# A message-passing layer with a sorted edge list: layernorm's products rebooked, the loop's vector work planned, gathers further ahead

## The chip, the cores and the metric

The kernel runs on one core of a Trainium2 chip. The metric is device microseconds (us) for one execution. TensorE is written PE here, VectorE DVE, ScalarE ACT, GpSimd POOL and SyncE SP. PE, DVE, ACT, POOL and SP each work through their own list of instructions in order; a semaphore makes one wait for another. The program order within each engine is the order in which the Python code emits the instructions.

## The reference

```python
h = jnp.maximum(_layernorm(x, axis=-1), 0.0)          # x: 6250 nodes x 128
feat = jnp.concatenate([h[dst], h[src] - h[dst]], axis=-1)
msg = feat @ W.T + b                                  # one message an edge, 206250 edges
out = jax.ops.segment_max(msg, dst, num_segments=6250)
x = x + jnp.where(jnp.isfinite(out), out, 0.0)
```

The edges are sorted by dst. They are two random lists of 100000, each with its reverse, and one loop edge a node. A message splits into a part of dst and a part of src, so the kernel computes two products a node (a part that is added to the output and the table Bt, which is to be maximised over a node's sources) and then takes the maximum of rows of Bt over each node's edges.

## The kernel before, in words

**Layout.** There are 128 lanes of 49 consecutive nodes (LD = 49). Each lane reads a window of 1792 edges (WIN), and nodes are also split as node = 50 l + q (Q = 50 and L = 125). Most of the edges are handled by matrix products with one-hots; those left over, edges whose (dst, q) occurs a second time in a lane, are handled as a stream of rows, 396 steps of 128 rows (GR = 396), one row a lane and step.

**Stage 1, loads (0 to 29 us).** The windows of src and dst are gathered, x is loaded in five groups of ten q (GQ = 10). `scaled` (L511) normalises two q on ACT into one of two buffers `hs`.

**Stage 2, the list's sums (29 to 109 us).** For 41 lags DVE compares each edge's key with that of the edge `lag` places before (L608), and PE adds the result into the PSUM tile `dup` (L597, four matmuls); five more sums mark edges before, in and behind the lane. Three buffers hold the compared lists, so DVE runs at most three ahead of PE. Into this the code strews layernorm: 75 parts (`micro`), three a pair of q: `turn` (transpose on PE, copy on ACT to `hT`, then normalise the next pair), `product` (a bias matmul and two f32 matmuls, L527 and L530, with two copies on ACT, L532 and L533) and `remainder` (one matmul L539, one copy L541, and for each fifth pair the store of Bt by SP, L545, and the adding store into out by POOL, L546). `ln(2)` emits two parts after each lag. `moments` and `scales` compute the statistics, `put_x` (L674) has SP copy raw x to out.

**Stage 3, marking and sorting (109 to 165 us).** ACT takes signs of `dup`, DVE scans them (L707), and eleven passes (`pass_`, L644 and L645: a test and a predicated copy) move the left-over edges to the front of each lane. Beside the passes the list `rest` says what is emitted after which pass: `turned` moves the three per-edge names into the layout of T3 (TQ, TD, TV), a quarter of the lanes at a time (14 or 28 matmuls of 32 columns, then a copy, L762); `build` compares names with row numbers into the first two units' homes (`pieces`, L203, L207, L210: six pieces a unit) and multiplies them into `pv` (`mats`, L242); `own_last` counts; `begin_rows` (after pass 7) computes the first indices `ridx` (L790) and issues LEAD = 16 row gathers. Then DVE closes the list, SP writes it to LT, POOL gathers from LT by `cols_` the rows that fuller lanes hand over, and DVE computes limits and checks.

**Stage 4, the loop (from 177 us).** A new pool takes over the memory of stages 1 to 3's pool. 13 tiles of ten lanes (490 columns; the last has 392) times 25 pairs of q give 325 pairs. A pair is: two to four one-hot products on PE (L955) turned into ones by ACT (L956), made one pair ahead; four or six f32 products into `ps` (L1046, two buffers); a maximum on DVE (L1052, or L1050 for a tile's first pair). `plan` holds, by tile and pair, the batches of `mats`, `feats` and `put_own` for the next tile, and `between` the pieces of the unit after the next. `more_rows` spreads the 396 steps of the row stream evenly over the first 291 pairs: a step (`stream_step`, L170) is a running maximum on DVE; after each, one more row is gathered (`gather_row`, L91) by POOL, made to wait for that step, so 16 rows are ahead; the ring in X holds 42 rows (GB = 7 groups of U = 6), and each full group is written by SP to M. From pair 112 on (`find_ends`), each third step also lets POOL gather a row R of ends out of M (32 by pair 291, 17 later). The last 34 pairs hold the finishing of the output.

## Time and profile before

| | us |
|---|---|
| median of three runs (805.58 to 807.24) | 806.66 |
| the profiled execution's own time | 804.5 |
| its span, first to last instruction | 802.8 |
| busy: PE, DVE, ACT, POOL | 684.5, 705.7, 554.7, 471.0 |
| mean granted clock of PE | 0.956 |

The profile lists, for one execution, when each instruction ran on its engine. A row of a timeline is: start, duration, engine, line, operation, output<-input, shape, count, and in brackets how long the engine sat idle before it and what released it. A row of a group has busy time and mean ns. A row of the waits is: who waited for whom, us in total, times, longest. PE's time is union time of overlapping matmuls, so a busy PE is not one at its peak.

### The profile page before, as it was taken

Reading aid. Unit: us, or ns where it says so; the run is one execution under the profiler, and the core shown is the slowest. Engines: PE = TensorE matmul, PEld = TensorE weight load, DVE = VectorE, ACT = ScalarE, POOL = GpSimd, SP = SyncE. Lnnn points to the kernel's source line nnn. Section 1 sums busy time; section 2 is a strip of 40 time slices with the busy share of each in tenths; the row PEclk is TensorE's granted clock in tenths of the full one; section 3 lists DMA queues with packets and bytes.
Section 4 is the critical chain, followed back from the end, with each engine's and each line's share of the span. In section 5 each row is a group of like instructions: output and inputs, shape, how many; then the busy total and the mean of one; then the engine's idle time right before and its main releaser. Section 6 shows DMA issues by size and latency. Waiting matters only on the chain.

```text
span 802.8 us, 12579 instructions
## 1 busy us (share of the span) xinstructions
PE 684.5 (85%) x3992; PEld 515.2 (64%) x3992; DVE 705.7 (88%) x1256; ACT 554.7 (69%) x1168; POOL 471.0 (59%) x519
## 2 busy tenths in 40 slices
PE   0599955509999899999989999999999989899995
PEld 0366635307767677776767777676777756667894
DVE  7997589937999898999989999999999888898885
ACT  4878942325887988889776776768676675666863
POOL 4001010363767676767767777777777777777372
PEclk9999977559999999999999999999999999999998
DMA  6845430021343343433333333333433333343137
GB/s 188 256 98 106 88 78 2 14 76 39 92 116 88 86 121 89 115 89 99 108 84 104 108 102 108 106 108 94 120 94 109 105 105 89 92 119 92 56 74 141
DMA packets 79653, 79.43 MB, mean 99 GB/s; under 512 B 10042, under 2 KB 68495, under 8 KB 79579
## 3 DMA queue, kind: packets, MB, share of 16 engines
q0 software_dynamic: 16560, 37.64, 18.5%
q1 hardware_dynamic: 62667, 40.30, 17.6%
q8 instruction: 33, 0.54, 0.3%
q10 hardware_dynamic: 352, 0.61, 0.3%
q14 instruction: 41, 0.34, 0.1%
HBM read 39.25 MB, written 39.19 MB: 98 GB/s over the span
## 4 chain that ended last, share of the span: by engine, by line
PE 44%; DVE 18%; ACT 13%; DMA 11%; issue 9%; POOL 3%; DVEq 0%; SPq 0%; POOLq 0%; ACTq 0%
PE ps L1046 22%; PE z L955 10%; DMA X<-Bt,ridx 8%; DVE acc L1052 7%; ACT oh L956 5%; PE pv L242 5%; DVE X L170 2%; PE dup L597 2%; POOL X L91 2%; PE pm L530 2%; DVE dwin L645 2%; ACT Vb L257 1%; ACT dump L1080 1%; DVE big L644 1%; ACT acc L533 1%
## 5 line engine op out<-in xcount | busy, mean ns | idle before, releaser
L91 POOL DMA_INDIRECT X<-Bt,ridx x396 | 390.7, 987 | 192.4 <-DVE X L170 59.5
L956 ACT ACTIVATE oh<-z 126x490 fp32r<-126x490 f32 (+1 forms) x754 | 381.7, 575 | 153.7 <-PE z L955 151.6
L1046 PE MATMUL ps<-oh,Bp 126*128 126x490 f32 (+1 forms) x1508 | 439.5, 419 | 19.1 <-DVE acc L1052 18.4
L1052 DVE TENSOR_TENSOR acc<-acc,ps 128x980 f32<-128x980 f32 (+1 forms) x312 | 359.8, 1153 | 38.0 <-PE ps L1046 34.1
L1046 PEld LDWEIGHTS ps<-oh,Bp 126*128 126x128 f32 x1508 | 281.4, 191 | 103.0 <-DVE acc L1052 43.4
L955 PE MATMUL z<-Vb,Sel 128*126 128x490 f16 (+1 forms) x650 | 195.3, 371 | 29.6 <-ACT oh L956 24.6
L170 DVE SCALAR_TENSOR_TENSOR X<-X,slim 128x128 f32<-128x128 f32 x395 | 136.2, 345 | 11.6 <-DMA X<-Bt,ridx 10.6
L955 PEld LDWEIGHTS <-Sel 128*126 128x126 f16 x754 | 99.4, 139 | 63.6 <-issue 29.7
L242 PEld LDWEIGHTS <-OHQ 128*128 128x128 bf16 x840 | 58.5, 161 | 19.3 <-issue 18.6
L203 DVE TENSOR_TENSOR OHQ<-T,IQ 128x1092 bf16<-128x1092 bf16 (+5 forms) x96 | 57.3, 600 | 12.4 <-DMA X<-LT,cols__1131 12.4
L242 PE MATMUL pv<-OHD,OHQ 128*128 128x28 bf16 (+1 forms) x826 | 62.2, 228 | 5.7 <-DVE OHD L210 5.7
L91 POOL DMA_INDIRECT R<-M,last_e x49 | 48.8, 995 | 20.0 <-issue 8.8
L546 POOL DMA_DIRECT2D out_x<-acc x10 | 8.5, 984 | 81.5 <-ACT Bp L541 42.8
L955 PE MATMUL z<-Vf,Sel 128*126 128x490 f16 (+1 forms) x104 | 38.7, 372 | 0.5 <-ACT Vf L257 0.5
L597 PE MATMUL dup<-T,identb 128*128 128x512 bf16 (+1 forms) x164 | 37.0, 353 | 0.0
L608 DVE TENSOR_TENSOR T<-KA,KB 128x1792 bf16<-128x1792 int16 x21 | 22.8, 1091 | 15.9 <-PE dup L597 15.9
L1080 ACT ACTIVATE dump<-lane_dl,nbias 128x472 bf16<-128x472 int32 x50 | 35.1, 702 | 0.1
L530 PE MATMUL pm<-wT,hT 128*125 128x256 f32 x100 | 26.2, 384 | 0.0
L597 PEld LDWEIGHTS <-identb 128*128 128x128 bf16 x164 | 15.1, 98 | 14.0
L511 ACT ACTIVATE hs<-X,nmr,rstd 125x128 f32<-125x128 f32 x50 | 22.4, 508 | 0.5 <-DMA M<-none 0.5
L608 DVE TENSOR_TENSOR T<-KA 128x1792 bf16<-128x1792 int16 x20 | 21.2, 1075 | 1.2 <-PE dup L597 1.1
L645 DVE COPY_PREDICATED dwin<-big,dwin 128x472 int32<-128x472 int32 (+10 forms) x12 | 21.8, 1818 | 0.4
(298 smaller groups left out, 511.8 us busy)
## 6 DMA issues: line engine op xcount, KB each, us to landing
M<-X SPq DMA_DIRECT2D x66, 384.0 KB
X<-Bt,ridx POOLq DMA_INDIRECT x396, 2.5
X<-in_x SPq DMA_DIRECT2D x5, 560.0 KB
out_x<-X SPq DMA_DIRECT2D x5, 560.0 KB
Bt<-acc SPq DMA_DIRECT2D x5, 560.0 KB
out_x<-acc POOLq DMA_DIRECT2D x5, 560.0 KB, 9.0
ownb<-Bt SPq DMA_DIRECT2D x11, 245.0 KB
out_x<-R POOLq DMA_DIRECT2D x5, 480.0 KB, 9.9
```

What stands on the lines that cost most here:

```text
L91: i = G_.indirect_dma_start(out=o, out_offset=None, in_=table, in_offset=bass.IndirectOffsetOnAxis(ap=idx, axis=0))
L170: step = V.scalar_tensor_tensor(G[:, j], state["prev"], slim[:, k:k + 1], G[:, j], op0=ALU.min, op1=ALU.max)
L203: V.tensor_tensor(OHQ[:, :nl, a:z], over(TQ, z - a), iq, ALU.is_equal)
L242: last = T_.matmul(o, w, m, start=False, stop=True, skip_group_check=True)
L530: T_.matmul(pm[:L, j], hT[k % 2][:, j, :L], wT, start=False, stop=j == 1)
L597: T_.matmul(dup[:, a:z], w, e[:, a:z], start=first, stop=last)
L608: V.tensor_tensor(e, KA[:, 64:], i1, ALU.is_equal)
L955: T_.matmul(z[:L + 1, :n], Sel[:, order[i // 2][j]], f[t % 2][:, :n], start=True, stop=True)
L956: A_.activation(oh[:, :n], z[:L + 1, :n], AF.Relu)
L1046: T_.matmul(ps[:, j, :n], w, o[:, :n], start=m == 0, stop=m == len(todo) - 1)
L1052: V.tensor_tensor(a, a, ps[:, :, :n], ALU.max)
L1080: A_.activation(dump, lane_dl, AF.Sign, scale=2.0, bias=nbias[:, c:c + 1], accum_out=ends[:, c:c + 1])
```

## The change

- **Bookings of layernorm.** Before, two parts follow each lag. After, one part comes ahead of the distances' absolute value and four ahead of the first sum; within the sums a budget of PE time (`ln_spare`, 0.15 us a lag and 0.3 to 2.0 us more at ten lags) decides; the rest come after ACT's signs (18) and after passes 0, 1, 2 (6, 8, 8) and 3 (what is left). Groups 1 to 4 are normalised in place in X, one pair a lag at most (`scale_more`), so `put_x` is emitted earlier. ACT's copies of swin and KA move to lags 3, 7 and 11; its copies of `dup` and of the names move behind the products.
- **Names.** `turned` now takes all 128 lanes at once, 14 blocks in the four banks of `dup`, with two copies; TD and TV after pass 4, TQ after pass 5. Clearing and the load of the first own rows come after pass 5, the four `own_last` after pass 6, both builds and the first features after passes 7 and 8. The homes of units 0 and 1 change places in `acc`.
- **Gathers.** LEAD is 20: three after pass 7, then one behind each DVE piece of the builds and passes 8 to 10. R0 is 32. In the loop a step gathers one row, each eighth step two, until 36 are ahead (AHEAD) or the ring is full.
- **Planned steps.** The code now keeps a reckoning of each engine's time (`tm`) from durations written in, and after each pair emits row steps and pieces until DVE's reckoned time meets PE's next pair; a row may be up to 12 ahead of its even spread if it is reckoned to have landed, and is forced when 5 behind.
- **Pools.** `cols_` moves to the pool that stays for the whole kernel. The first one-hots are emitted before the padding copies and the third unit's pieces. `handed` moves from pair 5 to pair 11.

```diff
-R0 = 24
+R0 = 32
-LEAD = 16
+LEAD = 20
+AHEAD = 36
...
+            cols_ = keep.tile([P, 1], I32, name="cols_")
...
-            at_ = 2 * (Q * (L + 1)) - (UL + TL - UL) * (SQ + WN) * NBLK
+            at_ = 2 * TL * LD
-            for u_ in (0, 1):
+            for u_ in (1, 0):
...
+                def normal(k):
+                    return hs[k % 2] if 2 * k < GQ else xs[:, 2 * k:2 * k + 2]
...
-                    if k + 1 < NP_:
+                    if 2 * (k + 1) < GQ:
                         scaled(k + 1)
+                def scale_more():
+                    if GQ <= 2 * ready["s"] < 2 * ready["n"]:
+                        scaled(ready["s"])
...
-                            micro.append((n, lambda f=f, n=n: f(n)))
+                            micro.append((n if f is turn else -1, lambda f=f, n=n: f(n),
+                                          {turn: 0.25, product: 1.15, remainder: 0.13}[f]))
...
+                def ln_spare(t):
+                    spare["pe"] += t
+                    while micro and spare["pe"] >= micro[0][2] / 2:
+                        n_ = len(micro)
+                        ln(1)
+                        if len(micro) == n_:
+                            break
                 scaled(0)
-                ln(1)
...
+                ln(1)
                 A_.activation(qn, q16, AF.Abs)
                 moments(GQ, GQ + GQ // 2)
                 V.tensor_tensor(KA[:, 64:], d128, qn, ALU.add)
-                A_.activation(s16, sq, AF.Identity, bias=nthr)
-                A_.activation(big, sq, AF.Copy, scale=float(1 << PB))
+                ln(4)
...
-                among[5] += [lambda: A_.copy(KB[:, 64:], KA[:, 63:63 + WIN])]
+                among[3] += [lambda: A_.activation(s16, sq, AF.Identity, bias=nthr)]
+                among[7] += [lambda: A_.activation(big, sq, AF.Copy, scale=float(1 << PB))]
+                among[11] += [lambda: A_.copy(KB[:, 64:], KA[:, 63:63 + WIN])]
...
-                    among[1 + 2 * j].append(put_x)
+                    among[(0, 1, 4, 8, 12)[j]].append(put_x)
...
-                    ln(2)
+                    scale_more()
+                    ln_spare(0.15 + {1: 0.7, 4: 1.4, 5: 1.4, 9: 1.4, 10: 0.3, 14: 1.4, 15: 1.4, 16: 2.0, 7: 0.8, 8: 0.8}.get(i, 0.0))
...
+                ln(18)
...
-                def turned(t, h, todo):
+                def turned(t, *todo):
+                    pt = dup.rearrange("p (j l) -> p j l", l=P)
+                    for a, z in ((0, 8), (8, NBLK)):
+                        for j in range(a, z):
+                            for m, (e, w) in enumerate(todo):
+                                T_.matmul(pt[:, j], e[:, j * P:(j + 1) * P], w, start=m == 0, stop=m == len(todo) - 1)
+                        A_.copy(t[:, :, a:z], pt[:, a:z].rearrange("p j l -> p l j"))
...
+                def paced(step):
+                    if state["gathered"] < LEAD:
+                        gather_row(step)
...
-                for i in range(6):
-                    rest[i] += [lambda: ln(2)]
-                    for a in turns[2 * i:2 * i + 2]:
-                        rest[i].append(lambda a=a: turned(*a))
-                rest[1] += [spread_a]
-                rest[3] += [spread_b, lambda: ln(len(micro)), clear_early, load_first]
-                rest[5] += [lambda: build(0)]
-                rest[6] += [lambda: build(1), lambda: own_last(0), lambda: own_last(1)]
-                rest[7] += [begin_rows, lambda: own_last(2), lambda: own_last(3), first_own]
+                rest[0] += [spread_0] + [lambda: ln(6)]
+                rest[1] += [lambda: ln(8)]
+                rest[2] += [lambda: ln(8), spread_a]
+                rest[3] += [lambda: ln(len(micro)), names]
+                rest[4] += [spread_b, lambda: turned(TD, (dlc, identb)), lambda: turned(TV, (vm, identb), (low, negL))]
+                rest[5] += [clear_early, load_first, lambda: turned(TQ, (dups, sgI), (name, halfI))]
+                rest[6] += [lambda: own_last(0), lambda: own_last(1), lambda: own_last(2), lambda: own_last(3)]
+                rest[7] += [begin_rows, lambda: build(0)]
+                rest[8] += [lambda: build(1), first_own] + [lambda j=j: feats(0, j) for j in range(6)]
...
-                at_pair(0, 5, handed)
+                at_pair(0, 11, handed, dve=1.4)
...
-                        at_pair(p, 0, lambda u_=p + 3: (between.extend(pieces(u_)), fill.update(most=6)))
+                        at_pair(p, 0, lambda u_=p + 3: (between.extend(zip(pieces(u_), (0.45, 0.45, 0.42, 0.42, 0.48, 0.58) if units[u_][1] == UL
+                                                                           else (0.32, 0.32, 0.3, 0.3, 0.35, 0.4))), fill.update(most=6)))
...
+                def one_row():
+                    step = stream_step()
+                    spend("dve", 0.265)
+                    for _ in range(1 + (state["ran"] % 8 == 0)):
+                        if state["gathered"] < min(state["ran"] + AHEAD, (state["ran"] // U + GB) * U, GR):
+                            gather_row(step)
+                            land.append(spend("pool", 1.26, tm["dve"]) + 2.0)
+                    if state["ran"] % 3 == 0:
+                        get_rows(1)
...
+                def fill_in(k):
+                    due = GR * (k + 1 - wait) / (span_ - wait)
+                    until = tm["pe"] + own_pe[k + 1]
+                    while len(between) > fill["most"]:
+                        one_piece()
+                    while state["ran"] < GR:
+                        n = state["ran"]
+                        if n < due - 5:
+                            one_row()
+                        elif tm["dve"] + 0.2 > until:
+                            break
+                        elif n < due + 12 and n < state["gathered"] and land[n] <= tm["dve"]:
+                            one_row()
+                        elif between:
+                            one_piece()
+                        else:
+                            break
...
-                    more_rows(GR * max(0, k + 1 - wait) // (len(pairs) - wait - early))
+                    fill_in(k)
```

More of the change, by code (lines that the diff above doesn't have):

```diff
@@ L690, in gnn_kernel @@
                 dups = s16.bitcast(BF16)
-                for a in range(0, WIN, 512):
-                    z = min(a + 512, WIN)
-                    A_.copy(dups[:, a:z], dup[:, a:z])
+                ln(18)
                 for r in range(2):
@@ L702, in gnn_kernel, with names @@
                 name = d16.bitcast(BF16)
-                A_.activation(name, q16, AF.Abs)
+                def names():
+                    for a in range(0, WIN, 512):
+                        z = min(a + 512, WIN)
+                        A_.copy(dups[:, a:z], dup[:, a:z])
+                    A_.activation(name, q16, AF.Abs)
                 for a in (0, HW):
@@ L713, in gnn_kernel @@
                 rows = pool.tile([1, 5, P + 2], F32, name="rows")
-                cols_ = pool.tile([P, 1], I32, name="cols_")
                 ovm = pool.tile([P, 1], F32, name="ovm")
@@ L753, in pass_ @@
                     for a, z in parts:
-                        move(i, a, z)
-                def turned(t, h, todo):
-                    h0, h1 = h * 32, h * 32 + 32
-                    pt = ps_t.tile([P, 32, NBLK], F32, name="ptb", tag="pt")
-                    for j in range(NBLK):
-                        for m, (e, w) in enumerate(todo):
-                            T_.matmul(pt[:, :, j], e[:, j * P:(j + 1) * P], w[:, h0:h1], start=m == 0, stop=m == len(todo) - 1)
-                    A_.copy(t[:, h0:h1], pt)
+                        step = move(i, a, z)
+                    return step
+                def turned(t, *todo):
[5 more added lines that the diff above has]
+                        A_.copy(t[:, :, a:z], pt[:, a:z].rearrange("p j l -> p l j"))
                 own_n = pool.tile([P, 4], F32, name="own_n")
@@ L791, in begin_rows @@
                                     op1=ALU.bitwise_and)
-                    for _ in range(LEAD):
+                    for _ in range(3):
                         gather_row()
@@ L902, in gnn_kernel, with spend, at_pair @@
                 fill = {"most": 6}
-                def at_pair(p, i, f):
-                    plan.setdefault((p // 2, i + 12 * (p % 2)), []).append(f)
+                tm = {"pe": 0.0, "dve": 0.0, "act": 0.0, "pool": 0.0}
+                land = [0.0] * LEAD
+                def spend(e, t, after=0.0):
+                    tm[e] = max(tm[e], after) + t
+                    return tm[e]
+                def at_pair(p, i, f, pe=0.0, act=0.0, dve=0.0):
+                    plan.setdefault((p // 2, i + 12 * (p % 2)), []).append((f, pe, act, dve))
                 for p in range(2 * NT):
@@ L960, in gnn_kernel @@
                 oh = one_hots(*pairs[0])
+                for o in OHQs:
+                    A_.copy(o[:, :, Q:].rearrange("p l q b -> p l (q b)"),
+                            zero[:, :(SQ - Q) * NBLK].rearrange("p (o n) -> p o n", o=1).to_broadcast([P, o.shape[1], (SQ - Q) * NBLK]))
+                for f in pieces(2):
+                    f()
+                spend("dve", 4.0)
                 acc2 = None
@@ L966, in gnn_kernel @@
                 wait, early = 2, 34
+                span_ = len(pairs) - early
+                own_pe = []
+                for k, (t, i) in enumerate(pairs):
+                    n = sum(len(x) for x in slots[i // 2])
+                    own_pe.append((n * 0.43e-3 + 2 * n * 0.457e-3) * cols[t] + sum(x[1] for x in plan.get((t, i // 2), ())))
+                own_pe.append(0.0)
                 def get_rows(limit):
@@ L1046, in gnn_kernel @@
                             T_.matmul(ps[:, j, :n], w, o[:, :n], start=m == 0, stop=m == len(todo) - 1)
+                    oh_next = tm["oh"]
+                    spend("pe", sum(len(x) for x in oh) * 2 * n * 0.457e-3, max(oh_at, tt_at[0]))
+                    tt_at = (tt_at[1], spend("dve", n * 2 / 0.96e3 + 0.07, tm["pe"]))
                     a = acc2[:, :, :n]
```

90 lines of the change are left out of this document (48 added, 42 removed).

## The prediction, made before the changed kernel ran

> **What bounds the kernel now.** I read the page first, then the busy time by stretches of the span, then the waits, and the timeline where a stretch looked odd. The first lines say that no engine is idle for long on average, which hides four stages with four limits.
>
> ```profile
> span 802.8 us, 12579 instructions
> ```
> ```profile
> PE 684.5 (85%) x3992; PEld 515.2 (64%) x3992; DVE 705.7 (88%) x1256; ACT 554.7 (69%) x1168; POOL 471.0 (59%) x519
> ```
>
> By stretches (length, then busy time and instruction count of PE, PEld, DVE, ACT, POOL, then the granted clock):
>
> ```profile
> 28.80:108.19 79.39, 76.13 (x380) 48.51 (x380) 61.48 (x144) 63.52 (x172) 8.47 (x10) 1.00 0.51 125
> 117.87:158.77 40.90, 23.49 (x371) 20.07 (x369) 39.94 (x49) 11.28 (x25) 4.90 (x4) 0.66 0.04 12
> 164.65:177.07 12.42, 0.00 (x0) 0.00 (x0) 0.00 (x0) 0.00 (x0) 9.13 (x10) 0.50 0.19 53
> 200.00:400.00 200.00, 189.87 (x1059) 143.68 (x1058) 186.26 (x316) 169.03 (x373) 140.76 (x144) 1.00 0.36 101
> 600.00:740.00 140.00, 128.19 (x709) 95.22 (x708) 123.53 (x204) 91.66 (x179) 107.09 (x109) 0.99 0.36 102
> ```
>
> The list's sums (28.8 to 108.2) are bound by PE: it is busy 76 of 79 us and DVE only 61. The sorting passes (117.9 to 158.8) are bound by DVE, 39.9 of 40.9 us, with PE half idle at a clock of 0.66. Then come 12.42 us in which only POOL works. In the loop all are close to full, so its stalls have to be read from the waits (who waited for whom: us in total, times, longest), here DVE in the sums, then PE and DVE in the loop:
>
> ```profile
> DVE T L608 <- PE dup L597: 17.0, 16, 1.6
> ```
> ```profile
> PE ps L1046 <- DVE acc L1052: 18.4, 26, 2.5
> PE pv L242 <- DVE OHD L210: 5.7, 7, 1.4
> ```
> ```profile
> DVE X L170 <- DMA X<-Bt,ridx: 10.6, 16, 1.2
> ```
>
> **The sums: layernorm's products taken out of PE's way.** Five sums (20 matmuls) run back to back at the stage's end, so a sum costs PE 0.81 us; four copies of ACT follow each product, one of 512 columns and three of 250 or 256, of which one row stands here.
>
> ```profile
> 104.12 4.04 PE L597 MATMUL dup<-T,identb 128*128 128x512 bf16 x20
> ```
> ```profile
> L533 ACT COPY acc<-pm 125x512 f32<-125x512 f32 x25 | 15.1, 603 | 0.0
> L541 ACT CAST Bp<-pm 125x256 fp32r<-125x256 f32 x25 | 9.8, 392 | 0.2
> ```
>
> 46 sums (41 lags and five more) are 37.2 us of PE's 76.1, so the 25 products take 38.9, 1.56 each. Followed line by line, the new bookings let out 34 of the 75 parts by the last sum (5 ahead of the sums, 29 among them); 41 stay: 18 behind the signs, 6, 8 and 8 behind passes 0 to 2, one behind pass 3. That is 12 products less, 18.7 us, and PE's 76.1 falls to 57.4, below DVE's 61.5. DVE becomes the bound and its 17.0 us of waits go, except where a booking of 1.4 to 2.0 us meets a short DVE stretch. I take 15 (10 to 17).
>
> Normalising in place costs no instruction: the twenty pairs of Relu only move earlier. Each must wait until the raw group has been copied out of X by SP's store; those five stores move up in SP's order (ahead of every store of Bt), and the first overwriting comes five sums after its store. Queued behind such a wait on ACT are the products' copies, and PE behind those. I cost it at nothing, covered by PE's spare 4 us (61.5 against 57.4); without the cover the 15 would shrink to the 10. The two copies of swin and the one to KB move later on ACT and are read only at sums 10, 16 and 20: nothing.
>
> **The passes: what the products now lie beside.** The twelve products cost PE 18.7 us, where it has 17.4 idle and turns names with 280 tiny matmuls that become 70 larger ones. The tight engine is ACT.
>
> ```profile
> 110.99 1.83 ACT L693 CAST s<-dup 128x512 bf16<-128x512 f32 x4
> 112.67 1.75 ACT L703 ACTIVATE d<-q 128x1792 bf16<-128x1792 bf16 x1
> ```
> ```profile
> 116.75 1.09 DVE L644 TENSOR_SCALAR big<-dwin 128x1791 int32<-128x1791 int32 x1
> ```
> ```profile
> L762 ACT CAST T<-ptb 128x448 bf16<-128x448 f32 x12 | 6.4, 532 | 14.0 <-PE ptb L761 14.0
> ```
>
> The first of these rows begins where ACT's signs end, 111.0, so at 96.0 after the first saving. Twelve products at 0.60 + 3 x 0.39 = 1.78 us are 21 us; with PE and ACT taking turns I take 2.0, 24 us, to 120. Then the names, 1.83 + 1.75, to 123.6. Turning TD, TV and TQ is 6.4 us of the same copies, and as all three pass through one PSUM tile, PE's matmuls stand between them; I take 9, to about 133. DVE comes to the first build after pass 7:
>
> ```profile
> 139.14 2.54 DVE L203 TENSOR_TENSOR acc<-T,IQ 128x1092 bf16<-128x1092 bf16 x4
> ...
> 143.15 1.05 DVE L644 TENSOR_SCALAR big<-dwin 128x1728 int32<-128x1728 int32 x1
> ```
> ```profile
> 146.42 1.81 DVE L203 TENSOR_TENSOR acc<-T,IQ 128x728 bf16<-128x728 bf16 x4
> ...
> 149.22 1.02 DVE L644 TENSOR_SCALAR big<-dwin 128x1664 int32<-128x1664 int32 x1
> ```
> ```profile
> 152.50 0.18 DVE L790 TENSOR_SCALAR ridx<-dwin 128x24 int32<-128x24 int32 x1
> ```
> ```profile
> 152.95 1.53 POOL L91 DMA_INDIRECT X<-Bt,ridx  x1 [38.19 <-DVE ridx L790]
> 154.79 1.59 POOL L91 DMA_INDIRECT X<-Bt,ridx  x1 [0.30 <-issue]
> ```
> ```profile
> 174.33 0.94 POOL L91 DMA_INDIRECT X<-LT,cols__1131  x1 [0.31 <-issue]
> 175.57 0.94 POOL L91 DMA_INDIRECT X<-Bt,ridx  x1 [0.30 <-issue]
> ```
> ```profile
> 177.07 2.55 DVE L203 TENSOR_TENSOR OHQ<-T,IQ 128x1092 bf16<-128x1092 bf16 x4 [12.42 <-DMA X<-LT,cols__1131]
> ```
>
> Before, 116.75 to 152.50 holds passes 0 to 7 and both builds (4.01 + 2.80 us); without them 28.9. After, passes begin at 101.8 and pass 7 ends at 130.7, so DVE waits some 2 us for TQ: I add 2 (0 to 8). What is moved past on SP (the load of the first own rows) and on POOL (the clearing of the homes, behind the last accumulating stores) has slack until then.
>
> **The change of pools.** In the last rows above DVE's wait names the gather from LT, indexed by cols_, behind sixteen row gathers: the loop's pool takes over the place in which cols_ stands. With cols_ in the pool that stays, the last user is DVE's own list of checks, which ended at 164.65. The whole 12.4 goes (0 to 12.4). First one-hots ahead of ACT's padding copies: DVE's own build of 4.0 us is then what pair 0 waits for, not PE; pair 0 came 5.4 after 177.07, so 1.4. The first maximum comes at 182.5 - 15 + 2 - 12.4 - 1.4 = 155.7.
>
> **The loop.** Its first maximum and its last streamed row:
>
> ```profile
> L1050 DVE TENSOR_TENSOR acc<-ps,acc x13: 975/1179/1180, 182.5 to 758.5; 128x980 f32<-128x980 f32 x12, 128x784 f32<-128x784 f32 x1
> ```
> ```profile
> L170 DVE SCALAR_TENSOR_TENSOR X<-X,slim x395: 333/344/417, 189.5 to 743.9; 128x128 f32<-128x128 f32 x198
> ```
>
> That is 561.4 us for 291 pairs, 11.64 tiles of 25, 48.2 a tile. What each engine needs, from a stretch where it runs without a gap:
>
> ```profile
> 286.18 1.06 PE L242 MATMUL pv<-OHD,OHQ 128*128 128x28 bf16 x14
> 287.08 0.61 PE L955 MATMUL z<-Vb,Sel 128*126 128x490 f16 x2
> ...
> 291.69 1.05 PE L242 MATMUL pv<-OHD,OHQ 128*128 128x28 bf16 x14
> ```
> ```profile
> 249.90 0.35 DVE L170 SCALAR_TENSOR_TENSOR X<-X,slim 128x128 f32<-128x128 f32 x1
> 250.17 1.17 DVE L1052 TENSOR_TENSOR acc<-acc,ps 128x980 f32<-128x980 f32 x1
> 251.25 0.34 DVE L170 SCALAR_TENSOR_TENSOR X<-X,slim 128x128 f32<-128x128 f32 x1
> ```
>
> PE: three pairs with one of the five batches of lane matmuls (0.90) take 5.51, so a tile takes 25 x 4.61 / 3 + 5 x 0.90 and about 0.6 of odd work, 43.5. DVE: 25 x 1.08, 34 rows at 0.27, builds of 6.8, 0.6 for the fold, 43.6. POOL: a gather each 1.24 to 1.25 us; 396 rows, one gather from LT and the 32 early ones of R are about 428, 535 us. Before they start at 152.95; after, once pass 7 is through (130.7), the last accumulating stores have landed and the homes are cleared:
>
> ```profile
> X<-Bt,ridx POOLq DMA_INDIRECT x396, 2.5
> ```
> ```profile
> out_x<-acc POOLq DMA_DIRECT2D x5, 560.0 KB, 9.0
> ```
>
> Products end about 121, two issues and 9.0 us of store make 132, clearing 133.8. So the rows can't end before 133.8 + 535 + 2.5 = 671, the bound by POOL, 46 us better than 561.4 after the same start.
>
> The plan adds no work. It touches three waits quoted above: PE for DVE's maximum (18.4) and for the last build (5.7), and DVE for a row that hasn't landed (10.6), 34.7 us; POOL, which now starts ahead and is told of 36 rows, is the way in which the last goes. It books a build at 0.45 to 0.58 and 0.30 to 0.40 us, 4.8 a tile, where the rows above say 6.8, so DVE will run later than booked and not every wait goes. I take four fifths, 28 us (0 to 46), 533.4. A gather that is told to come behind a DVE step holds up only other gathers on POOL, which are 20 and more ahead. Taking over rows from other lanes (`handed`) moves from pair 5 to pair 11, with the same instructions, long before row 260 needs them: nothing.
>
> **Sum.** 155.7 + 533.4 = 689.1 for the last row. The rest, 802.8 - 743.9 = 58.9, has its own limit (PE, 33 pairs and the stores) and is kept: a span of 748.0. The profiled execution took 804.5 at a span of 802.8, so 749.7; the median of 806.66 is 2.2 above that execution, so 752.
>
> **Rivals.** *The plan works fully*: POOL alone bounds, 671 + 58.9 + 3.9 = 734. For it: all three engines have under 44 us of work a tile. Against: three engines at one rate seldom fit without gaps.
> *The loop keeps its 48.2 a tile*: builds booked too low put DVE behind at each tile: 752 + 28 = 780. For it: the 2.0 us gap in the bookings. Against: 10.6 of the waits are for gathers, which start 19 us sooner.
> *The change of pools still waits* for the gather from LT, through another tile: that gather now has 20 rows ahead of it, 133.8 + 25 + 3.5 = 162.3, where DVE is through at 151.7: 752 + 10.6 = 763. The row names cols_, which speaks against it.
> *Slower*: the gathers are held up by a fuller DVE. Two gathers beside DVE's predicated copies took 1.53 and 1.59 us and came 1.84 apart. At that step 428 of them end at 133.8 + 788 + 2.5 = 924, and the time is 987. The kernel would be slower from a step of (806.7 - 133.8 - 2.5 - 58.9 - 3.9) / 428 = 1.42 us. Against it:
>
> ```profile
> L91 POOL DMA_INDIRECT X<-Bt,ridx x396 | 390.7, 987 | 192.4 <-DVE X L170 59.5
> ```
>
> a mean of 0.99 beside a DVE that is busy 93% of the loop already. The Trainium skill ("SBUF — State Buffer", section "SBUF: two separate sides") has the rule behind this rival: VectorE and GpSimd share one pair of ports under an exclusive lock, so DMAs whose descriptors GpSimd writes can stall behind some VectorE instructions. By that rule at its worst the time would be the 987 of this rival, by the loop's rows the 752 of the sum; the trace agrees beside the predicated copies (1.53, 1.59) and hardly in the loop (0.99).
>
> **How the numbers follow.** Forecast (740 to 768) 0.55, fully working 0.15, loop unchanged 0.15, change of pools still waiting 0.10, slower 0.05. The range 733 to 780 leaves out half of the first two rivals and the slower one. 0.2%, 1.6 us, is what the three runs (805.58 to 807.24) can tell from no change. All cases but the last are faster; for mixtures of the bad ones I leave 0.02 at no change: 0.94, 0.02, 0.04.
>
> **What would show it.** In the sums DVE's wait for PE should be under 3 us and the last sum near 93; DVE should wait little before the first build, near 131; no stretch before the loop in which only POOL works; first maximum near 156; about 45.8 us a tile, with PE's waits for the maximum and DVE's for rows near a fifth; gathers 1.25 apart. It is wrong if TQ comes over 8 us late, if another transfer holds the loop's pool, or if the tiles still take 48.

## The result, and the profile after

The changed kernel took 799.87 us (median of four runs, 797.71 to 800.41), the kernel before 806.95 beside it on the same chip (805.58 to 808.10): a ratio of 0.991, with an interval of 0.988 to 0.993. It is faster by 7 us, not by 55: the direction was right, and the time lies 20 us above my range. The profiled execution took 800.41 at a span of 798.6.

The page of the changed kernel, its span and busy time:

```profile
span 798.6 us, 12065 instructions
PE 694.1 (87%) x3776; PEld 513.2 (64%) x3782; DVE 724.7 (91%) x1256; ACT 552.6 (69%) x1162; POOL 476.2 (60%) x519
```

DVE runs the same 1256 instructions as before and is busy for 724.7 us, where it was 705.7: 19 us more for the same work. That is the first sign that something in their order has a price.

The stretches of the changed kernel, in the columns used before:

```profile
28.80:92.80 64.00, 56.84 (x265) 32.08 (x271) 61.77 (x146) 44.64 (x117) 3.51 (x4) 1.00 0.36 100
120.00:134.00 14.00, 8.92 (x43) 6.80 (x43) 0.38 (x5) 6.61 (x19) 2.72 (x5) 1.00 0.52 110
134.00:152.00 18.00, 10.22 (x75) 8.20 (x76) 12.66 (x12) 9.68 (x14) 5.32 (x7) 0.53 0.40 82
200.00:400.00 200.00, 187.68 (x1009) 139.15 (x1008) 187.50 (x303) 162.98 (x360) 147.59 (x149) 0.99 0.38 102
```

The sums are now DVE's (61.77 of 64.00). From 120 to 134 no engine is full: DVE 0.38 us of 14, PE 8.92, ACT 6.61. In the loop DVE does 303 instructions in the 200 us in which it did 316, and is no less busy.

The waits of DVE from 26 to 175 us, which cover sums, passes and the way into the loop:

```profile
DVE cols__105 L772 <- PE pm L768: 14.5, 1, 14.5
DVE acc L205 <- ACT T L796: 5.1, 1, 5.1
DVE T L636 <- PE dup L625: 1.5, 3, 0.9
```

The 17.0 us of waits in the sums are 1.5, as forecast, but two waits have come that were not there before, 14.5 and 5.1. The timeline has both (DVE, then the way into the loop):

```profile
133.58 0.16 DVE L772 CAST cols__105<-pm 128x1 int32<-128x1 f32 x1 [14.49 <-PE pm L768]
...
150.85 2.55 DVE L205 TENSOR_TENSOR acc<-T,IQ 128x1092 bf16<-128x1092 bf16 x4 [5.09 <-ACT T L796]
...
169.73 2.56 DVE L205 TENSOR_TENSOR OHQ<-T,IQ 128x1092 bf16<-128x1092 bf16 x4 [0.19 <-DVE badc L898]
...
173.69 1.17 DVE L1131 TENSOR_TENSOR acc<-ps,acc 128x980 f32<-128x980 f32 x1
```

L772 reads the counts that `spread_a` had PE multiply (L768); the first build (L205) waits for TQ. The stall of 12.42 us ahead of the loop is 0.19. The loop's first maximum is at 173.7, 18.0 later than the predicted 155.7. The loop's ends, by the first start of the maxima and the last of the rows:

```profile
L1131 DVE TENSOR_TENSOR acc<-ps,acc x13: 976/1179/1180, 173.7 to 753.0; 128x980 f32<-128x980 f32 x12, 128x784 f32<-128x784 f32 x1
```
```profile
L172 DVE SCALAR_TENSOR_TENSOR X<-X,slim x395: 333/352/417, 181.1 to 739.9; 128x128 f32<-128x128 f32 x198
```

The loop takes 739.9 - 173.7 = 566.2 us, where it took 561.4 and I expected 533.4. So the span splits against the prediction's 748.0: +18.0 up to the first maximum, +32.8 in the loop, -0.2 behind it, together the 50.6 that it is longer.

What the loop now looks like (DVE, at the end of a unit's pieces):

```profile
446.98 1.17 DVE L1133 TENSOR_TENSOR acc<-acc,ps 128x980 f32<-128x980 f32 x1
448.06 2.28 DVE L172 SCALAR_TENSOR_TENSOR X<-X,slim 128x128 f32<-128x128 f32 x6
451.19 1.18 DVE L1133 TENSOR_TENSOR acc<-acc,ps 128x980 f32<-128x980 f32 x1 [0.85 <-PE ps L1124]
452.81 1.18 DVE L1133 TENSOR_TENSOR acc<-acc,ps 128x980 f32<-128x980 f32 x1 [0.44 <-PE ps L1124]
453.91 1.51 DVE L172 SCALAR_TENSOR_TENSOR X<-X,slim 128x128 f32<-128x128 f32 x4
```

The plan emits rows in strings (six, four) and leaves pairs in which a maximum stands right behind a maximum. In the prediction's rows a row step cost 0.27 from its start to the next instruction's; here six take 2.28, 0.39 from one to the next.

### The profile page after: what moved, and what is told of

It is laid out like the page before. It is cut to its first block, busy times and chain, and to the rows that moved or that the text cites. A ratio compares the mean times of both kernels' runs of the same rounds, so it can differ in the third digit from the quotient of the medians.

```text
span 798.6 us, 12065 instructions
## 1 busy us (share of the span) xinstructions
PE 694.1 (87%) x3776; PEld 513.2 (64%) x3782; DVE 724.7 (91%) x1256; ACT 552.6 (69%) x1162; POOL 476.2 (60%) x519
## 4 chain that ended last, share of the span: by engine, by line
DVE 41%; PE 26%; issue 14%; ACT 12%; DMA 4%; DVEq 0%; POOL 0%; SPq 0%; ACTq 0%; POOLq 0%
DVE acc L1133 18%; PE ps L1124 12%; DVE X L172 8%; ACT oh L991 6%; PE z L990 6%; DVE OHQ L205 3%; PE pv L244 2%; DVE T L636 2%; DMA X<-Bt,ridx 2%; PE pm L547 2%; ACT dump L1163 1%; PE dup L625 1%; DVE dwin L673 1%; ACT Vb L259 1%; PE dup L795 1%
## 5 line engine op out<-in xcount | busy, mean ns | idle before, releaser
L92 POOL DMA_INDIRECT X<-Bt,ridx x396 | 395.9, 1000 | 134.6 <-issue 38.1
L990 PE MATMUL z<-Vb,Sel 128*126 128x490 f16 (+1 forms) x650 | 195.8, 373 | 11.3 <-ACT oh L991 6.6
L172 DVE SCALAR_TENSOR_TENSOR X<-X,slim 128x128 f32<-128x128 f32 x395 | 138.8, 351 | 8.4
L990 PEld LDWEIGHTS <-Sel 128*126 128x126 f16 x754 | 99.8, 140 | 46.5 <-issue 12.7
L563 POOL DMA_DIRECT2D out_x<-acc x10 | 9.2, 1129 | 109.2 <-ACT Bp L558 88.3
L244 PE MATMUL pv<-OHD,OHQ 128*128 128x28 bf16 (+1 forms) x826 | 61.8, 228 | 10.4 <-DVE OHD L212 10.4
L92 POOL DMA_INDIRECT R<-M,last_e x49 | 47.9, 978 | 18.9 <-issue 12.5
L205 DVE TENSOR_TENSOR OHQ<-T,IQ 128x1092 bf16<-128x1092 bf16 (+5 forms) x96 | 57.0, 602 | 0.2 <-DVE badc L898 0.2
L547 PE MATMUL pm<-wT,hT 128*125 128x256 f32 x100 | 28.3, 409 | 0.0
L544 PE MATMUL pm<-brow,bsel 128*125 128x512 f32 x25 | 13.2, 527 | 16.5 <-ACT Bp L558 14.6
L549 ACT CAST Bp<-pm 125x256 fp32r<-125x256 f32 x25 | 9.3, 371 | 25.6 <-PE pm L547 25.6
L547 PEld LDWEIGHTS pm<-wT,hT 128*125 128x125 f32 x100 | 20.4, 204 | 3.1
```

Of the source, the lines that this page charges most:

```text
L92: i = G_.indirect_dma_start(out=o, out_offset=None, in_=table, in_offset=bass.IndirectOffsetOnAxis(ap=idx, axis=0))
L172: step = V.scalar_tensor_tensor(G[:, j], state["prev"], slim[:, k:k + 1], G[:, j], op0=ALU.min, op1=ALU.max)
L205: return V.tensor_tensor(OHQ[:, :nl, a:z], over(TQ, z - a), iq, ALU.is_equal)
L244: last = T_.matmul(o, w, m, start=False, stop=True, skip_group_check=True)
L547: T_.matmul(pm[:L, j], hT[k % 2][:, j, :L], wT, start=False, stop=j == 1)
L990: T_.matmul(z[:L + 1, :n], Sel[:, order[i // 2][j]], f[t % 2][:, :n], start=True, stop=True)
```

## The experiments

Two things had to be explained: the start, 18.0 us late, and the loop, 32.8 us late. Eleven kernels ran. "Row behind row" and "maximum behind maximum" below are the mean or median time from the start of one to the start of the next where nothing of DVE's stands between, in the timeline from the first maximum to the last row. Loops are read from the two rows by line, as above. Each is one profiled execution, and the start moves it too: with the changed plan it is 562.8 to 566.2 in three kernels, with the even spread 552.9 to 556.4 in three, with the code of before 561.4 and 566.4 in two. A difference of under 5 us between loops with different starts therefore shows little.

**Rows without the plan.** The changed kernel with the old spread in place of `fill_in`: `even_rows`, whose body is left out here, emits rows up to the given count and a piece between two of them, as `more_rows` did before; a step still gathers as in the changed kernel.

```diff
-                    fill_in(k)
+                    even_rows(GR * max(0, k + 1 - wait) // (len(pairs) - wait - early))
```

> The changed kernel with the former rule of the loop put back: rows spread evenly over the pairs, a piece between two rows; gathers, pools and stages 1 to 3 stay as changed. Theory A (rows strung together): in the changed kernel 234 rows follow a row directly, start to start 0.388 us, against 0.266 when something else stands between, and 58 maxima follow a maximum at 1.27 and more, against 1.09; that is some 40 us of DVE. Without the strings the loop from first maximum to last row should fall from 566 to 525 to 540 us, the span to about 765. Rival B (the bookings of the pieces are too low, DVE falls behind, and nothing but that): the loop goes back to the 561 of before less the 10.6 of waits for gathers, 551. Rival C (all engines full, the order doesn't matter): 560 to 566.

Measured: 786.08 us, 0.973 (0.967 to 0.980) of before; the loop is 553.3, 12.9 shorter than with the plan. So the plan costs 13 us where I had it bring 28. Theory A had 26 to 41 us come off the loop and missed (525 to 540). Rival B's 551 came near by its number; its reason is tried by itself below. The rows of one behind another fall from 234 to 14. But an even spread with rows gathered up to 36 ahead is only 8.1 shorter than before's 561.4, and those 8 lie in tiles 9 to 11 (counted from 0: 46.9, 47.3 and 42.9 us for 49.7, 52.2 and 44.4). Waits between PE and DVE stay (DVE for PE 27.1 us, PE for DVE's maximum 13.6 from 180 to 705): both are near full (187.6 and 185.0 us of the 200 from 200 to 400) and each is late in other pairs.

**Strings put into the kernel before.** Rows emitted at each fourth pair, with no pieces among them.

```diff
-                        if n and between:
-                            between.pop(0)()
...
-                    more_rows(GR * max(0, k + 1 - wait) // (len(pairs) - wait - early))
+                    more_rows(GR * max(0, (k + 1) // 4 * 4 - wait) // (len(pairs) - wait - early))
```

> The kernel before, with its rows emitted after every fourth pair only, five or six in a row, and no piece between two rows; nothing else changed. Theory A (a row that follows a row directly costs 0.12 us more, as it needs the row before): some 310 rows follow a row, DVE has 35 to 40 us more to do, and the loop from first maximum to last row goes from 561 to 585 to 605 us. Rival B (strings cost nothing by themselves): 555 to 570.

Measured: 858.43 us, 1.063 (1.052 to 1.073); the loop is 613.2, 52 longer, more than expected. 322 rows stand behind rows at 0.387, 104 maxima behind maxima at 1.31, where a maximum with a row behind it takes 1.09. (322 - 14) x 0.12 = 37 us of DVE time are added by the rows alone. The maxima behind maxima may add up to 104 x 0.22 = 23 more, though for most of these the last to come was PE's product. Rows bunched at every fourth pair also make PE wait: its waits for DVE's maximum go from 18.4 to 44.3 in the loop. So strings are shown to be dear without any of the change, but how much of the 52 is the strings' own price and how much the bunching, this run can't tell.

**The same strings, two chains.** Is it that a row reads what the row before it wrote, or only that two of one form stand together? Here each row takes its maximum with the row two before, so the running maximum falls into two and the output is not the reference's; sizes and order stay.

```diff
-                if state["prev"] is not None:
-                    step = V.scalar_tensor_tensor(G[:, j], state["prev"], slim[:, k:k + 1], G[:, j],
+                if k > 1:
+                    step = V.scalar_tensor_tensor(G[:, j], ring((k - 2) // U)[:, (k - 2) % U], slim[:, k:k + 1], G[:, j],
```

> The changed kernel, but each row step takes its running maximum from the row two before instead of from the row just written (the running maximum falls into two interleaved ones, so the output is not the reference's; every instruction is as large and in the same order). Theory D (a vector instruction that reads what the one before it wrote starts 0.12 us later): row behind row falls from 0.388 to about 0.27 us start to start, maximum behind maximum stays at 1.27 to 1.41; some 27 us of DVE's loop go, of which PE leaves 10 to 20: 780 to 790. Rival F (two instructions of one form in a row cost this, whatever they read): 0.388 stays, and the time is 799 to 801.

Measured: 785.90 us, 0.975 (0.966 to 0.983). Row behind row falls to 0.274 (233 of them); the loop is 549.6, 16.6 shorter. The same two strings as above, in DVE's timeline of this run:

```profile
439.82 1.67 DVE L172 SCALAR_TENSOR_TENSOR X<-X,slim 128x128 f32<-128x128 f32 x6
441.68 2.49 DVE L1133 TENSOR_TENSOR acc<-acc,ps 128x980 f32<-128x980 f32 x2 [0.20 <-PE ps L1124]
444.09 1.13 DVE L172 SCALAR_TENSOR_TENSOR X<-X,slim 128x128 f32<-128x128 f32 x4
```

Six rows take 1.67 where they took 2.28, four 1.13 where they took 1.51. Theory D holds: it is the dependence. A row takes 0.35 us; behind a row that it reads it starts 0.04 after that one's end, here 0.08 before it. The two maxima, 2.49 for both, still stand 1.3 apart. Each reads the accumulator that the one before wrote, and by the semaphores in the changed kernel's trace 46 of its 59 such maxima waited last for the maximum before, so the same reason is likely, but no run took that dependence away.

**The bookings alone.** The prediction blamed pieces booked too low (4.8 a tile for 6.8) for what the plan would miss.

```diff
-                        at_pair(p, 0, lambda u_=p + 3: (between.extend(zip(pieces(u_), (0.45, 0.45, 0.42, 0.42, 0.48, 0.58) if units[u_][1] == UL
-                                                                           else (0.32, 0.32, 0.3, 0.3, 0.35, 0.4))), fill.update(most=6)))
+                        at_pair(p, 0, lambda u_=p + 3: (between.extend(zip(pieces(u_), (0.62, 0.62, 0.59, 0.59, 0.68, 0.68) if units[u_][1] == UL
+                                                                           else (0.43, 0.43, 0.4, 0.4, 0.48, 0.48))), fill.update(most=6)))
```

> The changed kernel with only the bookings of the pieces mended (0.62, 0.59, 0.68 for the larger unit, 0.43, 0.40, 0.48 for the smaller); rows may still stand behind rows, 210 times where the changed kernel has 234, maximum behind maximum 52 where it has 76. Theory S (the strings are the loss): little changes, 790 to 799. Rival B (the low bookings are the loss, as my prediction's rival had it): most of the 17 us that the mended plan brought beside the third buffer comes without the ban on strings too, 781 to 786.

Measured: 802.01 us (791.27 to 803.12), 0.990 (0.981 to 0.999). The time itself settles little, since the start, where this kernel's code is the same as the changed one's, went 8.0 us slower in the profiled run (last section). The loop alone can be compared: 560.7, 5.5 shorter than 566.2 and 2.1 shorter than the shortest loop of the same plan (562.8, with the third buffer), with 210 rows still behind rows at 0.386 and 34 maxima behind maxima for 59. Rival B wanted most of 17 us. The low bookings are a small part, 2 to 5.5 us, and some of that may come of the fewer strings.

**The plan mended.** This kernel has the third buffer of the run after the next one as well. Its plan has the mended bookings, no row behind a row unless rows are late and no piece is left, and something behind every maximum where there is anything.

```diff
-                    while len(between) > fill["most"]:
-                        one_piece()
-                    while state["ran"] < GR:
+                    last = "max"
+                    while True:
                         n = state["ran"]
-                        if n < due - 5:
+                        row = n < GR and n < state["gathered"] and n < due + 4 and land[n] <= tm["dve"] + 0.5
+                        late = n < GR and n < due - 4
+                        if last != "row" and (row or late):
+                            if last == "piece" and not late and len(between) <= fill["most"] and tm["dve"] + 0.2 > until:
+                                break
                             one_row()
-                        elif tm["dve"] + 0.2 > until:
-                            break
-                        elif n < due + 12 and n < state["gathered"] and land[n] <= tm["dve"]:
+                            last = "row"
+                        elif between and (len(between) > fill["most"] or late or last == "max" or tm["dve"] + 0.4 < until):
+                            one_piece()
+                            last = "piece"
+                        elif late:
+                            spend("dve", 0.12)
                             one_row()
-                        elif between:
-                            one_piece()
```

> The changed kernel with three PSUM buffers for products, and with the plan of the loop kept but mended: pieces booked at 0.40 to 0.68 us, as measured, a row never directly behind a row when a piece is to be had (10 such pairs of rows instead of 234), and something after each maximum. Theory A (the strings of rows and of maxima are what the plan lost): the loop from first maximum to last row takes 535 to 550 us, under the 553 of the even spread, and the span is 752 to 768. Rival C (no order of DVE's list helps below the even spread, since PE and DVE are each full in turn in different pairs): 553 to 560.

Measured: 765.23 us, 0.948 (0.942 to 0.953); the loop is 543.9, 22.3 shorter than the changed kernel's, 18.9 shorter than with the third buffer alone (562.8) and 9.0 shorter than the even spread on the same start (552.9, below). That is theory A's 535 to 550. 10 rows stand behind rows and one maximum behind a maximum. DVE's timeline of this run, at a stretch in which pieces are left:

```profile
424.87 1.18 DVE L1137 TENSOR_TENSOR acc<-acc,ps 128x980 f32<-128x980 f32 x1 [0.62 <-PE ps L1128]
425.96 0.35 DVE L172 SCALAR_TENSOR_TENSOR X<-X,slim 128x128 f32<-128x128 f32 x1
426.23 1.17 DVE L1137 TENSOR_TENSOR acc<-acc,ps 128x980 f32<-128x980 f32 x1
427.31 0.35 DVE L172 SCALAR_TENSOR_TENSOR X<-X,slim 128x128 f32<-128x128 f32 x1
427.57 0.72 DVE L205 TENSOR_TENSOR OHQ<-T,IQ 128x1092 bf16<-128x1092 bf16 x1
```

One row between two maxima serves both: row to maximum 0.27, maximum to row 1.08.

**The counts earlier.** For the start, the first theory was PE's order: the matmuls of `spread_a` (L768) stood behind all the parts that follow passes 0, 1 and 2. Here it is emitted ahead of those after pass 1, 16 parts earlier.

```diff
-                rest[1] += [lambda: ln(8)]
-                rest[2] += [lambda: ln(8), spread_a]
+                rest[1] += [spread_a, lambda: ln(8)]
+                rest[2] += [lambda: ln(8)]
```

> The changed kernel with spread_a, whose small matmuls DVE waits for at L772, moved from behind pass 2 to the front of what follows pass 1, so that on PE 16 parts fewer stand ahead of it. Theory P (order in PE's list alone): the 14.5 us wait of DVE goes and the first maximum comes at about 159 instead of 173.7. Rival Q (the products after the sums take 2.58 us each and end near 134 whatever is ahead): DVE waits for TQ at the first build instead, 13 to 18 us, and the first maximum comes 2 to 5 us earlier only, at 169 to 172.

Measured: 805.51 us, 0.999 (0.996 to 1.003), no gain. The wait at L772 is gone, and the first build waits that much longer and more. The first maximum is at 178.3, later than either theory had it and 4.6 later than in the changed kernel; PE's granted clock was also lower here, 0.73 from 120 to 134 where the changed kernel had 1.00, and the two shares of the 4.6 can't be told apart. The wait of DVE between 26 and 180, and what held PE:

```profile
DVE acc L205 <- ACT T L796: 24.9, 1, 24.9
```
```profile
113.50 0.80 PE L768 MATMUL pm<-ones,rows 1*128 1x1 f32 x6 [0.94 <-issue]
120.30 0.79 PE L544 MATMUL pm<-brow,bsel 128*125 128x512 f32 x1 [6.00 <-DVE jump L776]
```

PE's next product waited 6.00 us until DVE had read the counts out of their tile, which is one of the two `pm` buffers. The order was not the cause; the products themselves were late, and anything else in a `pm` buffer makes them later.

**A third buffer for the products.** `ps_m` gets three buffers, `ps_t` one.

```diff
-ps_t = pre.enter_context(tc.tile_pool(name="ps_t", bufs=2, space=PSUM))
+ps_t = pre.enter_context(tc.tile_pool(name="ps_t", bufs=1, space=PSUM))
...
-ps_m = pre.enter_context(tc.tile_pool(name="ps_m", bufs=2, space=PSUM))
+ps_m = pre.enter_context(tc.tile_pool(name="ps_m", bufs=3, space=PSUM))
```

> The changed kernel with three PSUM buffers for products and one for transposes, instead of two and two. Theory Q (PE waits for ACT's last copy of the product before the last, as two buffers are all it has): the step from product to product after the sums falls from 2.58 us to 1.8 to 2.0, the thirteen end some 8 us earlier, and the first maximum comes at 163 to 167 instead of 173.7. Rival P (only the order of PE's list): the step stays, first maximum at 173 to 174. If one transpose buffer is too few, the sums get longer by some us.

Measured: 782.76 us, 0.969 (0.963 to 0.976). The first maximum is at 160.2, 13.5 earlier. How the products follow each other on ACT, in the changed kernel:

```profile
97.14 0.37 ACT L549 CAST Bp<-pm 125x256 fp32r<-125x256 f32 x1 [1.18 <-PE pm L547]
...
99.73 0.37 ACT L549 CAST Bp<-pm 125x256 fp32r<-125x256 f32 x1 [1.18 <-PE pm L547]
...
102.31 0.37 ACT L549 CAST Bp<-pm 125x256 fp32r<-125x256 f32 x1 [1.17 <-PE pm L547]
```

and with the third buffer:

```profile
98.62 0.37 ACT L549 CAST Bp<-pm 125x256 fp32r<-125x256 f32 x1 [0.31 <-PE pm L547]
...
100.06 0.37 ACT L549 CAST Bp<-pm 125x256 fp32r<-125x256 f32 x1
...
101.66 0.37 ACT L549 CAST Bp<-pm 125x256 fp32r<-125x256 f32 x1 [0.19 <-PE pm L547]
```

A product every 2.58 us with ACT idle for 1.18 of it, against one every 1.4 to 1.6, less than the 1.8 to 2.0 of theory Q. Only while the tile of `spread_0` (L754, until DVE reads it at L758) holds one of the three, four steps from 103 to 113, does it go back to 2.5 to 2.6. DVE's wait at L772 is gone; one of 6.6 us at the first build is left.

**The rest of the parts.** Only `cols_` moved to the lasting pool, in the kernel before:

```diff
+            cols_ = keep.tile([P, 1], I32, name="cols_")
...
-                cols_ = pool.tile([P, 1], I32, name="cols_")
```

> The kernel before with one edit: cols_ stands in the pool that stays. Theory R (the loop's pool waited for the gather that reads cols_, and for nothing else): the 12.4 us in which only POOL works go, DVE's first build of the loop follows its checks by under 1 us, and the whole is 10 to 12.4 us shorter, about 796. Rival S (the rows gathered early, or the gather from LT itself, are late next): the first rows are waited for instead, and 0 to 5 us are gained.

Measured: 795.19 us, 0.985 (0.979 to 0.990). The first maximum moves from 182.5 to 169.8, 12.7 earlier; the 12.42 are gone with this line. In the profiled run the loop takes 566.4 and gives 5.0 of it back. DVE's waits in that loop are longer by nearly as much: 33.6 for PE and 11.3 for rows, where before's loop has 29.8 and 10.6. Why PE came later is not settled.

The third buffer with the even spread, and the same with a larger budget in the sums:

```diff
-                    ln_spare(0.15 + {1: 0.7, 4: 1.4, 5: 1.4, 9: 1.4, 10: 0.3, 14: 1.4, 15: 1.4, 16: 2.0, 7: 0.8, 8: 0.8}.get(i, 0.0))
+                    ln_spare(0.25 + {1: 0.7, 4: 1.4, 5: 1.4, 9: 1.4, 10: 0.3, 14: 1.4, 15: 1.4, 16: 2.0, 7: 0.8, 8: 0.8}.get(i, 0.0))
```

> The changed kernel with three PSUM buffers for products and the former even spread of rows. If the two faults lie apart (products after the sums, strings in the loop), the gains add: first maximum near 160, loop near 553, time about 769. If they share a cause, or the earlier start moves POOL's gathers into the way, it stays above 775.

> The same as e7 with 0.25 instead of 0.15 us of PE booked after each lag, so that two or three products more are done within the sums. If PE has the spare 4 to 7 us there that its busy time shows, the sums stay within 1 us, DVE's 6.6 us of waiting for TQ shrink to under 3, and the time falls by 3 to 5 us against e7. If the sums are already bound by PE and ACT taking turns, the sums get 3 to 4 us longer and nothing is gained.

Measured: 773.77 (0.958, 0.955 to 0.962), then 770.24 (0.954, 0.951 to 0.956). The first has its maximum at 158.7 and its loop at 552.9, as expected if the two faults lie apart. With the budget of 0.25, eleven products are left behind the sums for fourteen, and DVE's wait for TQ falls from 6.5 to 0.7; the first maximum moves from 158.7 to 152.3, and the loop gives 3.5 of it back (552.9, 556.4).

Last, the mended plan, the third buffer and the budget together:

> The mended plan (no row behind a row, pieces booked at what they take), the third buffer for layernorm's products and the larger budget in the sums (0.25 for 0.15). If the parts add: 765.2 of the mended plan with the third buffer, less the 3.5 that the budget brought beside the even spread: 760 to 763. Rival: what the start gains is lost again in the loop's first tiles, where gathers can't start sooner, 765.

Measured: 756.98 us (756.18 to 758.18), 0.938 (0.934 to 0.943) of before and 43 us below the changed kernel. The parts add, and a little more: first maximum at 152.3, loop 545.2. On the same start the mended plan's loop is 11.2 shorter than the even spread's (556.4). It is the fastest of all that ran.

```profile
L1135 DVE TENSOR_TENSOR acc<-ps,acc x13: 976/1179/1180, 152.3 to 710.4; 128x980 f32<-128x980 f32 x12, 128x784 f32<-128x784 f32 x1
```
```profile
L172 DVE SCALAR_TENSOR_TENSOR X<-X,slim x395: 333/346/410, 155.9 to 697.6; 128x128 f32<-128x128 f32 x198
```

The loops side by side:

| kernel | row behind row | maximum behind maximum | loop, us |
|---|---|---|---|
| before | 14 at 0.38 | 3 | 561.4 |
| before, `cols_` moved | 14 at 0.40 | 3 | 566.4 |
| after | 234 at 0.39 | 59, median 1.27 | 566.2 |
| after, counts earlier | 234 at 0.39 | 59, median 1.27 | 563.2 |
| after, third buffer | 234 at 0.39 | 59, median 1.27 | 562.8 |
| after, two chains | 233 at 0.27 | 59, median 1.28 | 549.6 |
| after, bookings mended | 210 at 0.39 | 34, median 1.28 | 560.7 |
| after, even spread | 14 at 0.38 | 3 | 553.3 |
| after, third buffer, even spread | 14 at 0.38 | 3 | 552.9 |
| after, third buffer, budget, even spread | 14 at 0.38 | 3 | 556.4 |
| after, third buffer, plan mended | 10 at 0.39 | 1 | 543.9 |
| after, third buffer, budget, plan mended | 10 at 0.38 | 1 | 545.2 |
| before, strings | 322 at 0.39 | 104, median 1.31 | 613.2 |

## Why the prediction was wrong, point by point

**The sums: right.** ACT's signs begin at 92.8 where they began at 109.2, 16.4 earlier for 15; DVE is the bound.

**The change of pools: right.** The stall went whole (12.42 to 0.19), pair 0 waits for DVE's build alone (169.7 to 173.7) as booked, and the kernel with that one line shows that it is this line. The rival that the pools still wait fell.

**The passes: wrong by 18.** Two sizes in "with PE and ACT taking turns I take 2.0, 24 us, to 120" failed. The twelve was miscounted: the 34 parts that I had by the last sum hold eleven products, so fourteen of the 25 stay, and from the signs on there were fourteen copies of 512 columns (L550). And a step took 2.58, not 2.0. With two buffers PE can't begin the next product until ACT has copied the remainder (L558) of the product before the last, which ACT does only behind its copies of the last; ACT then waits 1.18 for PE to finish the next. I added up ACT's copies (1.78) and looked at no buffer. Thirteen steps of 2.58 and one hold-up of 3.4, in which `spread_0`'s tile was in a buffer, are the 37 us from the signs' end at 94.6 to the last product at 131.5; PE comes to L768 at 132.8, and ACT to the names at 134.2 instead of 120. The "2 (0 to 8)" of waiting became 14.5 + 5.1 = 19.6, of which I had booked 2; the difference is 17.6 of the 18.0. That 14.5 stand at L772 and not at the build only says which reader of PE's late work comes first: with that reader moved ahead, the build waited 24.9. Turning the names took from 137.5 to 150.8, 13 us for the 9 that I took, at a clock of 0.53.

**The loop: wrong by 33.** The step that failed is "The plan adds no work". It adds no instruction, but it puts (234 - 14) rows behind rows, 0.12 dearer each, 27 us of DVE time, and 59 maxima behind maxima, some 0.19 dearer each, 11 us. DVE was as full as PE (187.5 and 187.7 us of the 200 from 200 to 400), so 16.6 of the 27 show in the loop (two chains), and most of the rest came back as waits of DVE for PE (24.0 us for 15.8 from 180 on). I had read 0.27 for a row and 1.08 for a maximum from a stretch in which they alternate, and used them for an order in which they don't.

What is left of the 32.8, some 16, is the second half of that step: "I take four fifths". The changed kernel's rows for the three waits (DVE for a gathered row has none):

```profile
PE ps L1124 <- DVE acc L1133: 11.4, 32, 2.5
PE pv L244 <- DVE OHD L212: 10.4, 10, 2.5
```

So 21.8 of the 34.7 us are left and 12.9 went, not 28; the wait for the last build grew from 5.7 to 10.4 instead of shrinking, and with the bookings mended it is 11.7. Nor does a wait that goes come off the loop in full. With the even spread 13.6 and 5.1 are left, 16.0 less than before, and the loop is 8.1 shorter; with the mended plan 4.8 and 6.9 are left, 23.0 less, and it is 17.5 shorter. In the rest PE and DVE, each busy over 92% of 200 to 400, wait for each other in turn. The rival "the loop keeps its 48.2 a tile" was the nearest on the loop, for another reason than it gave: the bookings it named are worth 2 to 5.5.

On one point the Trainium skill bears on this. "VectorE: DVE Perf Modes", section "The DRAIN you can't avoid", says that leaving out the semaphores of a chain of vector instructions doesn't save the emptying of the pipeline between them: eight copies took the same time both ways. The same section says that a next instruction which is not held starts earlier. The trace agrees with the second: a row starts 0.39 us after the start of a row that it reads and 0.27 after that of one that it doesn't, same instruction, same place, only the operand changed. Whoever takes the first by itself would price a row the same wherever it stands; the measurement decides.

**The gathers: right but for their start.** They begin at 146.0, not at 133.8, as pass 7, which gives them their indices, came late by the wait at L772. They run up to 36 ahead and DVE no longer waits for rows (10.6 before). The slower rival did not come: a gather lasts 1.00 us in the mean, for 0.99 before (one, beside the passes, took 3.98):

```profile
L92 POOL DMA_INDIRECT X<-Bt,ridx x396 | 395.9, 1000 | 134.6 <-issue 38.1
```

**The tail: right**, 58.7 for 58.9. The last kernel, with both causes mended, comes near the forecast (757.0 for 752.0), but by luck as far as the forecast goes: it has a third buffer and another plan, which the forecast kernel had not, and its terms differ. Its first maximum is at 152.3 for 155.7, its loop 545.2 for 533.4.

## What to carry to other kernels

When a plan reorders the work of a full engine, price each instruction by its neighbour: one that reads what the instruction before it wrote cost 0.12 us more here than one that has something else between, so alternate two chains rather than finish one. Don't count a wait that goes as time that goes: here 23.0 us of waits less made a loop 17.5 shorter. When work moves beside other work, count its buffers: two engines that hand tiles over through two buffers, one of which others borrow, ran at 2.58 a step where three gave 1.4 to 1.6, and one borrowed buffer cost 3.4 more. And a stall that moves when its instruction is moved, without the end moving, is a symptom: look for what its engine was late with.

## What the runs showed of the hardware that was not expected

**The clock in the passes differs between executions of the same code.** The kernel with the bookings alone took 801.59 to 803.12 us in three executions with a mean granted clock of 0.949 to 0.951, and 791.27 in one with 0.970. Up to the loop it is the changed kernel. PE's timeline, the bias matmul of a product (L544), first in the changed kernel:

```profile
110.88 0.79 PE L544 MATMUL pm<-brow,bsel 128*125 128x512 f32 x1 [1.83 <-DVE rows L758]
...
114.60 0.50 PE L544 MATMUL pm<-brow,bsel 128*125 128x512 f32 x1 [0.66 <-ACT Bp L558]
```

then in the kernel with the bookings alone:

```profile
110.13 0.79 PE L544 MATMUL pm<-brow,bsel 128*125 128x512 f32 x1 [1.87 <-DVE rows L758]
...
113.85 0.79 PE L544 MATMUL pm<-brow,bsel 128*125 128x512 f32 x1 [0.59 <-ACT Bp L558]
...
121.29 0.79 PE L544 MATMUL pm<-brow,bsel 128*125 128x512 f32 x1 [0.59 <-ACT Bp L558]
```

In the same gap of 1.8 to 1.9 us both fall to half speed (0.50 to 0.79 us a matmul); one is back after one product, the other goes on at half speed, granted 0.50 from 120 to 134 where the first has 1.00, and its first maximum is at 181.7 instead of 173.7. The Trainium skill ("TensorE: Matmul & The Clock Gate", section "Part 1: The HAM clock gate") says that the window in which activity is judged runs freely, so that the same kernel warms up at different points from run to run; this agrees. Here a stage in which PE is half idle ended 8 us apart for the same code, so the loop has to be compared by itself.

**Dependent vector instructions cost more in two forms**: 0.12 us for a row of 128 columns (0.27 to 0.39), some 0.19 for a maximum of 980 (1.08 to 1.27); the second is not proved to be the dependence.
